# Row sums of a graph-attention kernel's exponentials: eight matmul tiles of 64 rows by 32 columns in two PSUM banks, in place of four of 128 rows by 32

## The chip, the cores and the metric

The kernel runs on one core of one Trainium2 chip. The metric is the device time of one execution in microseconds (us); lower is better. The time before is the median of three runs, and one further execution was taken by the hardware profiler.

## The reference

Two graph layers over x (8 batches, 2048 nodes, 256 features) with one adjacency matrix (2048 x 2048). Everything is float32. What matters here is the first layer's attention: softmax is taken separately inside each chunk of 256 keys, and the weighted values of the eight chunks are added.

```python
# layer 0, on h = relu(layernorm(x)); q, k, v in 4 heads of 64
scores = einsum('bhnd,bhjcd->bhnjc', q, kc) / sqrt(64)     # j: 8 chunks, c: 256 keys
scores = where(mask == 0, -10, clip(scores, -10, 10))
attn = softmax(scores, axis=-1)                            # over the 256 keys of a chunk
ctx = einsum('bhnjc,bhjcd->bhnd', attn, vc)
out = layernorm(ctx @ Wo.T + bo + h) * gamma + beta        # x = x + out
# layer 1, on h = relu(layernorm(x)): additive attention over all 2048 keys, then x = x + elu(...)
```

## The kernel before

One function, `layers`, writes the instructions of both layers in an order laid down by hand; each engine then runs its own queue in that order, and semaphores tie the queues together. Work beside the main line (projections, transposes, layer norms) is held in generators, and `advance` and `tick` hand a few of them out per step. So the place of an instruction in its queue is fixed when the program is built.

**The steps of the first layer.** There are 256 steps: 8 batches, 4 blocks of 512 queries, and 8 pairs of a 512-key block and a pair of heads. A 512-key block holds two chunks of 256 keys (`c` = 0 and 1), and is worked in four parts `t`; in a part, rows 0 to 63 of a tile are 64 keys of chunk 0, rows 64 to 127 are 64 keys of chunk 1. The loop at the end works on step n, n+1 and n+2 at once, in the order `S0 E0 S1 E1 C0 S2 E2 M0 C1 S3 E3 C2 C3 B0 A0`:

- S (`scores`, matmul L529): the scores of step n+2, four matmuls on 64x64 quarters of the TensorE array, into a `pair` of PSUM banks; then VectorE clips and masks them into `E` (L537). E (`exponential`, L543) is the exponential on ScalarE.
- C (`weigh`, matmul L551): step n's exponentials times the values, again on 64x64 quarters, into the banks `both`.
- A: `add_up` (matmul L564) takes the sum over keys of step n+1's exponentials, which GpSimd has first added over the four parts (`added`, L921 and L923) into one tile of 128 rows; `divide` copies the sums out of PSUM on ScalarE (L575) and sends them with a small DMA into 128 partitions (L577, tile `sum`).

After the order, `accumulate` multiplies step n's weighted values with the reciprocal sums `r` on VectorE (L603, L605), `invert` takes the reciprocals for step n+1 (L582) and writes them to DRAM (`inv`, L584), `spread` reads them back to all partitions (`r`, L591), and `advance` emits work beside it: mostly `narrow` (L162, four 32-column tiles over all 128 rows) or transposes (`flip`, L171).

**The sums before the change.** A matmul names a tile of the array by the partitions of its operands and of its output. In `add_up` four matmuls use all 128 rows and 32 columns each, for two heads times two halves of 256 queries. Their weights are `both_of`, 128 x 32: rows 0 to 63 have ones in columns 0 to 15, rows 64 to 127 in columns 16 to 31, so that one tile keeps the two chunks apart. The eight wanted rows come out at partitions 0, 16, 32 and so on of one bank (`sums`, 128 x 256), and L577 takes every sixteenth row. A float32 matmul appears in the trace as two weight loads and two matmuls.

The second layer (from L981 on) uses 32-column tiles of 128 rows (L1003, L1014) and has no part in the change.

Of the kernel before, what the change touches and what calls it, by code (L numbers as in the profile page):

```python
# [8 lines left out]
F32 = mybir.dt.float32  # L9
# [7 lines left out]
P = 128  # L17
# [34 lines left out]
def layers(  # L52
# [18 lines left out]
    nc = tc.nc  # L71
# [12 lines left out]
    big = ctx.enter_context(tc.tile_pool(name="big", bufs=2))  # L84
# [10 lines left out]
    def pair(dtype=F32):  # L95
        n = QB if dtype == F32 else 2 * QB
        return psum.tile([P, 2, n], dtype, tag="big", name="big", bufs=3)

    def banks(name):
        return [psum.tile([P, QB], F32, tag=f"both{k}", name=name) for k in range(2)]  # L100
# [5 lines left out]
    def heads_tile(name, tag, bufs=2):  # L106
        return big.tile([P, 2, QB], F32, tag=tag, name=name, bufs=bufs)
# [10 lines left out]
    def fetch_all():  # L118
        while loads:
            nc.sync.dma_start(*loads.pop(0))  # L120
# [99 lines left out]
    def advance(all_of=True):  # L220

        moved = all_of and tick()
        for steps_of in list(aside):
            got = next(steps_of, aside)
            if got is aside:
                aside.remove(steps_of)
            moved = moved or got is not False
            if got is None:
                break
        return moved  # L230

    def drain(until=lambda: False):
        while not until() and advance():
            pass
# [178 lines left out]
    def batch(b):  # L413
        qkv[b] = ([], [], [])
        rstd, off = norm_of[b] = norms()
        mv = small.tile([P, NKT, 2], F32, tag="mv", name="mv", bufs=1)
        ready, turned = [], []

        def slot():

            n = here[0]
            while b and here[0] < n + 1:
                yield False

        def statistics():

            for blk in range(NQB):
                while (
                    here[0] < first_of(b) + slot_of(b, TURN[blk]) - (5 if b > 1 else 7) or len(turned) < blk
                    if b  # L430
                    else blk > len(turned) + 2
                ):
                    yield False
                xb = load(x[b], blk)
                if b == 0:
                    fetch_all()
                yield True
                for two in range(NT // 2):
                    yield from slot()
                    for t in (2 * two, 2 * two + 1):  # L440
                        row_stats(nc, small, mv[:, blk * NT + t, :], xb[:, t, :])
                roots(mv, rstd, off, slice(blk * NT, (blk + 1) * NT))
                yield from slot()
                ready.append(xb)

        quiet.append(statistics())
        if b == 0:
            yield from opening(ready, turned)
            return
        hTs = {}  # L450
        for blk in range(NQB):
            yield from turning(b, blk, ready, turned, hTs)
            for name in "qkv" if blk == 2 else "kvq":
                yield from item(b, name, blk, hTs[blk], *qkv[b])
# [50 lines left out]
    def bias():  # L505
        spread_bv = big.tile([P, 2, P], F32, tag="h", name="spread_bv", bufs=3)
        nc.vector.tensor_copy(spread_bv, bcast(bv_col, 2, P))
        yield from later()
        ps = aux()[:, :F]
        for s in range(2):  # L510
            nc.tensor.matmul(
                ps, spread_bv[:, s, :], wT["o"][:, s, :], start=(s == 0), stop=(s == 1)
            )
        nc.vector.scalar_tensor_tensor(brow["o"], ps, float(NCH), brow["o"], ALU.mult, ALU.add)
        yield

    both_of = const.tile([P, 32], F32, tag="both_of", name="both_of")
    nc.gpsimd.memset(both_of, 0.0)
    for c in range(2):
        nc.gpsimd.memset(both_of[64 * c : 64 * c + 64, 16 * c : 16 * c + 16], 1.0)  # L520

    def scores(qb, blk, t, hp, qs, ks):

# [21 lines left out]
    def weigh(hp, t, e, v, both):  # L545

        for hh in range(2):
            mine = slice((2 * hp + hh) * DH, (2 * hp + hh + 1) * DH)
            for c in range(2):
                own = slice(64 * c, 64 * c + 64)  # L550
                nc.tensor.matmul(  # L551
                    both[c][64 * hh : 64 * hh + 64, :],
                    v[own, t, mine],
                    e[own, hh, :],
                    start=(t == 0),
                    stop=(t == NT - 1),
                )

    def add_up(added, sums):

        for hh in range(2):
            for half in range(2):
                n = 2 * hh + half
                nc.tensor.matmul(  # L564
                    sums[32 * n : 32 * n + 32, :],
                    both_of,
                    added[:, hh, half * 256 : (half + 1) * 256],
                    start=True,
                    stop=True,
                )  # L570

    def divide(sums):

        s = big.tile([P, 256], F32, tag="s", name="s", bufs=1)
        nc.scalar.copy(s, sums)  # L575
        got = small.tile([P, 16], F32, tag="sum", name="sum")
        nc.sync.dma_start(got, s[0:P:16, :].rearrange("n (j i) -> n j i", i=16))  # L577
        return got

    def invert(got):  # L580
# [303 lines left out]
    def fill(qb):  # L884

        while here[0] < (B - 1) * NQB * NCH + qb * NCH + NCH - 1:
            yield False
        for two in range(NKT // 2):
            fill_pair(qb, two)
            yield True  # L890

    def last_batch():
        yield from batch(B - 1)
        aside.append(sources_of(W, a))
        yield from preparation(0)
# [5 lines left out]
    def mask_part():  # L901
        next(mask_compares, None)
        next(mask_turns, None)

    def prepared(step):


        b, qb, c = step
        blk, hp = divmod(c, 2)
        drain(lambda: (qb, blk // 2) in made and b in qkv and len(qkv[b][1]) > blk and len(qkv[b][0]) > qb)  # L910
        qs, ks, _ = qkv[b]
        for t in range(NT):
            e = scores(qb, blk, t, hp, qs, ks)
            yield e
            exponential(e)
            yield None
# [11 lines left out]
    for n in range(-2, len(steps)):  # L928
        here[0] = n
        if n >= 0:  # L930
            b, qb, c = steps[n]
            blk, hp = divmod(c, 2)
            if n == NT:
                aside.append(bias())
            b1 = 1 if n == 1 else b + 2 if (qb, c) == (NQB - 1, NCH - 2) else B
            if b1 < B:
                aside.append(batch(b1) if b1 + 1 < B else last_batch())
            if b == B - 1 and c == NCH - 2 and qb < NQB - 1:
                aside.append(fill(qb))
            drain(lambda: len(qkv[b][2]) > blk)  # L940
            both = banks("both")
            v = qkv[b][2][blk]
        coming = prepared(steps[n + 2]) if n + 2 < len(steps) else iter(())
        inside = -1 <= n < len(steps) - 1
        weights[n + 2] = []
        for kind, t in ORDER:
            if kind in "SE":
                weights[n + 2] += [e for e in (next(coming, None),) if e is not None]
            elif kind == "A":
                if inside:  # L950
                    sums = pair()[:, 0, :256]
                    add_up(totals.pop(n + 1), sums)
                    got = divide(sums)
            elif kind == "B":
                if 0 <= n < 4:
                    advance(False)
            elif kind == "M":
                mask_part()
            elif n >= 0:
                weigh(hp, t, weights[n][t], v, both)  # L960
        weights.pop(n, None)
        if n + 2 < len(steps):
            totals[n + 2] = added(weights[n + 2])
        if n >= 0:
            if c == 0:
                accs[qb] = heads_tile("acc", "acc")
            accumulate(accs[qb][:, hp, :], both, r, blk == 0)
            if c == NCH - 1:
                finish(b, qb, accs[qb])
        held = invert(got) if inside else None  # L970
        if n >= 0:
            tick()
        if inside:
            r = spread(held)
        fetch_all()
        for _ in range({-2: 5, 3: 2}.get(n, 3 if n < NQB * NCH else 2)):
            advance(n < 0)
        mask_part()
# [204 lines left out]
    for s, (k, jt) in enumerate(rounds):  # L1183
# [44 lines left out]
        for entry in [entry for entry in due if entry[0] <= s]:  # L1228
            due.remove(entry)
            _, j, blocks = entry  # L1230
# [296 lines left out]
```

## Time and profile before

| what | value |
|---|---|
| time, median of 3 runs (lowest to highest) | 3971.54 us (3970.2 to 3981.95) |
| profiled execution: time; span from first to last instruction | 3974.03 us; 3972.2 us |
| busy share of the span: PE, DVE, ACT, POOL | 97%, 86%, 64%, 85% |
| mean granted TensorE clock | 0.992 |
| first and last matmul of L564 | 49.1 us, 2586.2 us |
| L564: instructions, mean of one | 2048, 392 ns |
| L575, copy of the sums: instructions, mean of one | 256, 366 ns |

PE is TensorE's matmuls, PEld its weight loads, DVE is VectorE, ACT ScalarE, POOL GpSimd, SP SyncE, which issues DMAs. A matmul's end is modelled, so the distance between the starts of matmuls tells more than their busy time. A line "A <- B" means that A waited for B or reads B. The chain of waits is followed back from the last instruction, at each step to what released it.

### The profile page before, as it was taken

The numbers are of one execution on the slowest core, as the hardware profiler recorded it, in microseconds if no ns is written. First come the engines' busy times: TensorE is split into PE (matmuls) and PEld (weight loads), VectorE is DVE, ScalarE is ACT, GpSimd is POOL, SyncE is SP. The second block draws the span as 40 slices with busy tenths as digits, with TensorE's granted clock in tenths as the row PEclk, the third lists the DMA queues.
The fourth block names the chain that finished last, engine by engine and source line by source line (L and its number), as shares of the span: only waits on it lengthen the run. The fifth ranks groups of instructions, "written<-read, shape, count | busy, mean of one in ns | idle before, by whom it ended". The sixth has DMA issues, their size and how long they took to land.

```text
span 3972.2 us, 93255 instructions
## 1 busy us (share of the span) xinstructions
PE 3846.7 (97%) x38454; PEld 1359.6 (34%) x38454; DVE 3409.6 (86%) x3920; ACT 2527.0 (64%) x3635; POOL 3380.8 (85%) x1763
## 2 busy tenths in 40 slices
PE   7899999999999999999999998989999999999997
PEld 2233333333333333333333333323333333333332
DVE  5778888888888888888888877879999999999998
ACT  7756556666566566656665656556766667676666
POOL 4678899999899899999999988858778778788887
PEclk9999999999999999999999999999999999999999
DMA  7723333333333333333333333322223122232222
GB/s 184 175 74 82 82 82 88 82 83 93 83 82 85 84 84 82 90 84 80 86 90 81 77 91 84 88 75 78 57 66 76 47 74 67 55 72 62 55 55 50
DMA packets 379442, 324.33 MB, mean 82 GB/s; under 512 B 261504, under 2 KB 329856, under 8 KB 379008
## 3 DMA queue, kind: packets, MB, share of 16 engines
q1 hardware_dynamic: 373312, 301.24, 29.8%
q0 software_dynamic: 4608, 16.78, 1.2%
q8 instruction: 304, 4.98, 0.5%
q14 instruction: 130, 1.06, 0.1%
q10 hardware_dynamic: 1088, 0.26, 0.0%
HBM read 271.26 MB, written 36.18 MB: 77 GB/s over the span
## 4 chain that ended last, share of the span: by engine, by line
PE 64%; DMA 13%; DVE 9%; POOL 5%; ACT 4%; issue 3%; SPq 1%; DVEq 0%; POOLq 0%; ACTq 0%
PE acc L1003 17%; PE big L529 15%; PE both L551 13%; PE big L162 7%; PE den L1014 6%; DMA r<-inv 5%; POOL t L1214 3%; DMA sum<-s 3%; DMA inv<-sum 3%; DVE E L537 3%; PE rest L162 2%; PE big L564 2%; DVE e L993 2%; ACT E L543 2%; DMA x<-in_x_dram 2%
## 5 line engine op out<-in xcount | busy, mean ns | idle before, releaser
L543 ACT ACTIVATE E<-E 128x1024 f32<-128x1024 f32 x1024 | 1081.8, 1058 | 683.1 <-DVE E L537 623.8
L537 DVE SCALAR_TENSOR_TENSOR E<-big,limit 128x1024 f32<-128x1024 f32 x1024 | 1198.6, 1214 | 91.5 <-PE big L529 85.9
L923 POOL TENSOR_TENSOR add<-add,E 128x1024 f32<-128x1024 f32 x512 | 1216.3, 2376 | 40.3 <-ACT E L543 0.2
L993 DVE SCALAR_TENSOR_TENSOR e<-near,far,limit 128x2048 f32<-128x2048 f32 x512 | 1166.6, 2341 | 30.7 <-issue 16.1
L529 PE MATMUL big<-qT,kT 64*64 64x512 f32 x8192 | 1069.6, 601 | 34.7 <-DVE E L537 11.8
L551 PE MATMUL both<-E,v 64*64 64x512 f32 x8192 | 1075.1, 592 | 9.4 <-DVE acc L605 6.2
L1214 POOL TENSOR_TENSOR t<-t,e 128x1024 f32<-128x1024 f32 x384 | 911.7, 2420 | 188.3 <-PE den L1014 99.7
L1003 PE MATMUL acc<-e,qn 128*32 128x512 f32 x8192 | 979.1, 595 | 11.8 <-DVE e L993 11.6
L921 POOL TENSOR_TENSOR add<-E 128x1024 f32<-128x1024 f32 x256 | 629.2, 2458 | 209.1 <-ACT E L543 208.7
L1173 ACT ACTIVATE t<-e,quot 128x1024 f32<-128x1024 f32 x384 | 419.8, 1141 | 200.3 <-PE den L1014 148.8
L551 PEld LDWEIGHTS both<-E,v 64*64 64x64 f32 x8192 | 341.8, 134 | 588.0 <-issue 502.1
L529 PEld LDWEIGHTS big<-qT,kT 64*64 64x64 f32 x8192 | 293.6, 133 | 613.0 <-issue 342.8
L1003 PEld LDWEIGHTS acc<-e,qn 128*32 128x32 f32 x8192 | 270.6, 110 | 554.9 <-issue 467.6
L603 DVE TENSOR_TENSOR both<-both,r 128x512 f32<-128x512 f32 x448 | 310.8, 694 | 165.1 <-DMA r<-inv 118.9
L605 DVE TENSOR_TENSOR acc<-both,acc 128x512 f32<-128x512 f32 x448 | 309.8, 692 | 15.3
L1014 PE MATMUL den<-t,for_sums 128*32 128x512 f32 x1536 | 230.6, 593 | 7.7 <-POOL t L1214 7.6
L564 PE MATMUL big<-add,both_of 128*32 128x256 f32 x2048 | 164.0, 392 | 0.0
L1014 PE MATMUL den<-e,for_sums 128*32 128x512 f32 x1024 | 149.9, 592 | 0.0
L582 DVE RECIPROCAL sum<-sum 128x16 f32<-128x16 f32 x256 | 63.7, 249 | 87.8 <-DMA sum<-s 83.8
L162 PE MATMUL big<-hT,wk 128*32 128x512 f32 x1024 | 125.1, 610 | 9.9 <-ACT hT L179 9.9
L1131 ACT ACTIVATE z<-z,dens 128x64 f32<-128x64 f32 x496 | 124.6, 334 | 2.0 <-DVE z L1115 2.0
L162 PE MATMUL big<-wv,hT 128*32 128x256 f32 x2048 | 123.5, 383 | 1.4 <-ACT hT L179 1.3
(142 smaller groups left out, 3060.7 us busy)
## 6 DMA issues: line engine op xcount, KB each, us to landing
r<-inv SPq DMA_DIRECT2D x512, 256.0 KB
x<-in_x_dram SPq DMA_DIRECT2D x96, 512.0 KB
es<-er SPq DMA_DIRECT2D x64, 512.0 KB
adj_in<-in_adj_dram SPq DMA_DIRECT2D x32, 512.0 KB
x<-o POOLq DMA_DIRECT2D x32, 512.0 KB, 4.4
x<-x SPq DMA_DIRECT2D x32, 512.0 KB
xh<-x SPq DMA_DIRECT2D x128, 128.0 KB
out_dram<-xh SPq DMA_DIRECT2D x124, 128.0 KB
```

The lines of the kernel that those rows point to most:

```text
L162: nc.tensor.matmul(to[32 * j : 32 * j + 32], lhsT[:, n : n + 32], rhs, start=start, stop=stop)
L529: nc.tensor.matmul(ps[64 * c : 64 * c + 64, hh, :], ks[blk][own, hp, keys : keys + 64], qs[qb][own, hp, :], start=True, stop=True,)
L537: nc.vector.scalar_tensor_tensor(e, ps, -0.5, bcast(limit[:, qb, NT * blk + t, :], 1, 2), ALU.max, ALU.min)
L543: nc.scalar.activation(e, e, AF.Exp, scale=0.25 * EDGE)
L551: nc.tensor.matmul(both[c][64 * hh : 64 * hh + 64, :], v[own, t, mine], e[own, hh, :], start=(t == 0), stop=(t == NT - 1),)
L921: nc.gpsimd.tensor_tensor(total, tiles[0], tiles[1], ALU.add)
L923: nc.gpsimd.tensor_tensor(total, total, e, ALU.add)
L993: nc.vector.scalar_tensor_tensor(e, near, far[:, jt, h : h + 1], limit[:, :, jt, :], ALU.max, ALU.min)
L1003: nc.tensor.matmul(acc[part][32 * blk : 32 * blk + 32, :], qn[jt // NT][:, jt % NT, own], e[:, blk, :], start=(jt == 0), stop=(jt == NKT - 1),
L1014: nc.tensor.matmul(den[32 * blk : 32 * blk + 32, :], for_sums[:, jt, :], blocks[blk], start=first, stop=last,)
L1173: nc.scalar.activation(t, e[:, 2 * half : 2 * half + 2, :], AF.Copy, scale=shared[b][4][:, jt // 2, h : h + 1],)
L1214: nc.gpsimd.tensor_tensor(ts[half], ts[half], now[:, 2 * half : 2 * half + 2, :], ALU.add)
```

## The change

`both_of` becomes all ones. Each of the four matmuls of `add_up` becomes two, one for each chunk: 64 rows of weights and of data, 32 columns, the same 256 columns of data, and the two row halves write two different banks of the pair. `divide` copies both banks (512 elements a partition in place of 256), and the DMA takes every thirty-second row, which now holds both chunks.

```diff
     both_of = const.tile([P, 32], F32, tag="both_of", name="both_of")
-    nc.gpsimd.memset(both_of, 0.0)
-    for c in range(2):
-        nc.gpsimd.memset(both_of[64 * c : 64 * c + 64, 16 * c : 16 * c + 16], 1.0)
+    nc.gpsimd.memset(both_of, 1.0)
...
                 n = 2 * hh + half
-                nc.tensor.matmul(
-                    sums[32 * n : 32 * n + 32, :],
-                    both_of,
-                    added[:, hh, half * 256 : (half + 1) * 256],
-                    start=True,
-                    stop=True,
-                )
+                for c in range(2):
+                    own = slice(64 * c, 64 * c + 64)
+                    nc.tensor.matmul(
+                        sums[32 * n : 32 * n + 32, c, :],
+                        both_of[own, :],
+                        added[own, hh, half * 256 : (half + 1) * 256],
+                        start=True,
+                        stop=True,
+                    )
...
-        s = big.tile([P, 256], F32, tag="s", name="s", bufs=1)
-        nc.scalar.copy(s, sums)
+        s = big.tile([P, 512], F32, tag="s", name="s", bufs=1)
+        nc.scalar.copy(s.rearrange("p (c q) -> p c q", c=2), sums)
         got = small.tile([P, 16], F32, tag="sum", name="sum")
-        nc.sync.dma_start(got, s[0:P:16, :].rearrange("n (j i) -> n j i", i=16))
+        nc.sync.dma_start(got, s[0:P:32, :].rearrange("n (j i) -> n j i", i=16))
...
-                    sums = pair()[:, 0, :256]
+                    sums = pair()[:, :, :256]
```

The rows of `got` and of everything behind it stay as they were. On each engine the order of the instructions stays the same too, but for the four matmuls that become eight and two memsets fewer on GpSimd.

## The prediction

> **What bounds the kernel now.** I read the busy shares and the chain of waits first, then the first layer alone, because L564 runs only from 49 to 2586 us.
>
> ```profile
> PE 3846.7 (97%) x38454; PEld 1359.6 (34%) x38454; DVE 3409.6 (86%) x3920; ACT 2527.0 (64%) x3635; POOL 3380.8 (85%) x1763
> PE 64%; DMA 13%; DVE 9%; POOL 5%; ACT 4%; issue 3%; SPq 1%; DVEq 0%; POOLq 0%; ACTq 0%
> 60.00:2600.00 2540.00, 2471.05 (x24829) 892.96 (x24824) 2097.90 (x3043) 1561.79 (x2004) 2261.83 (x1186) 0.99 0.34 89
> by line: PE big L529 23.0%; PE both L551 20.8%; PE big L162 10.6%; DMA r<-inv 8.0%; DMA inv<-sum 4.2%; DMA sum<-s 4.2%; DVE E L537 3.7%; issue 3.4%; PE big L564 3.2%; ACT E L543 2.5%; DVE both L603 2.2%; DMA x<-in_x_dram 2.1%; DVE acc L605
> ```
>
> The third line is the window 60 to 2600 us (span, then busy time of PE, weight loads, DVE, ACT, POOL); the fourth is the chain inside it. TensorE is busy for 2471 of 2540 us, so it has at most 69 us of slack, and over half of the chain lies on it. Most of the rest of the chain is the path of the sums: the small DMA into `sum`, the one to `inv`, and the reading of `r`. Time added to TensorE therefore mostly reaches the end; so does time added to the path of the sums, in those steps where that path is the late one.
>
> The next view is the one the forecast rests on: one pass of L564 and its neighbours in the timeline of PE.
>
> ```profile
> 1001.51 0.61 PE L529 MATMUL big<-qT,kT 64*64 64x512 f32 x4
> 1001.94 1.90 PE L551 MATMUL both<-E,v 64*64 64x512 f32 x16
> 1003.77 0.64 PE L564 MATMUL big<-add,both_of 128*32 128x256 f32 x8
> 1004.23 1.91 PE L162 MATMUL big<-wo,acc 128*32 128x256 f32 x32
> 1006.07 0.66 PE L171 MATMUL big<-ident,h 128*128 128x128 f32 x4
> ```
>
> Four matmuls run at once and start as a burst. From the first line to the second, one burst of 512 columns takes 0.43 us, so one of 256 columns takes 0.215. L551 has four bursts, 1.72 us, and would end at 1003.66; L564 starts at 1003.77, 0.11 late, though nothing it needs is late. Its own two bursts should take 0.43 and take 0.46. L162 then follows with no loss: its eight bursts would end at 1005.95. L171 starts at 1006.07, again 0.12 late. Time is lost where the tile's form changes (64x64 to 128x32, then 128x32 to 128x128), and not between L564 and L162, which share one form. In the trace's records the medians from start to start are 539 ns from L551's last burst to L564 against 429 inside L551 (110 lost), 330 from L564 or L162 to L171 against 216 (114 lost), 329 from L162 to L529's 64x64 (113 lost), and 202 from L171 to L529 against 109 (93 lost). The weight loads say why:
>
> ```profile
> 1003.77 0.16 PEld L564 LDWEIGHTS big<-add,both_of 128*32 128x32 f32 x8 [0.81 <-issue]
> 1004.01 0.35 PEld L162 LDWEIGHTS big<-wo,acc 128*32 128x32 f32 x8
> ```
>
> L162's weights load at 1004.01, under L564's second burst and 0.22 us before their own matmul. L564's load only at 1003.77, with the matmul. A change of form thus empties the array and bares a load: 240 ns instead of 216 for the first burst, 24 more.
>
> **What the change removes and adds on TensorE.** Before, a pass has the form change 64x64 to 128x32 ahead of it. Behind it come L162 or L791 (also 128x32) in 228 of 256 passes, counted in the trace, and another form in the other 28. After, 64x64 goes to 64x32, and 64x32 to 128x32.
>
> - Entry: 64x64 to 64x32 changes the columns alone. The nearest row is the change of columns alone from 128x32 to 128x128, which costs 114 ns, as much as the changes of rows and columns together. Bounds 0 and 114; I take 110 plus 24, as before. Difference 0.
> - Exit, 228 passes: 64x32 to 128x32 changes the rows alone, which no row shows. Every change that is shown costs 93 to 114, so bounds 0 and 114; I take 114, and 24 for L162's first load. In the other 28 it is paid before and after.
> - Streaming: eight tiles of half the height are the whole array, so 16 matmuls still need two rounds of 256 columns, 0.43 us. Two things could spoil that. The rate of issue: the change needs 16 matmuls in 0.43 us, and L791, in the fence below, issues 16 in four bursts 0.109 apart (medians of the starts), the same rate. And the two row halves writing two banks at once: L529 already does so with 64x64 tiles. I take 0; the upper bound, four tiles at a time, is 0.43 a pass.
> - Start: four tiles begin 0.02 us apart in all (a burst of L529 spans 0.61 where one matmul has 0.59), about 7 ns each. In a stream of one form this hides; ahead of a form change the last tile's end counts. Four more tiles: 0.027 us.
>
> ```profile
> 2465.53 0.62 PE L791 MATMUL big<-hT,wa 128*32 128x128 f32 x16
> L575 ACT COPY s<-big 128x256 f32<-128x256 f32 x256 | 93.7, 366 | 5.5 <-PE big L564 5.3 <-ACT E L543 0.2
> L357 ACT COPY v<-big 128x512 f32<-128x512 f32 x64 | 36.8, 577 | 47.6 <-PE big L162 47.6
> L179 ACT COPY hT<-big 128x512 f32<-128x512 f32 x72 | 41.9, 583 | 79.5 <-PE big L171 79.3
> DVE both L603 <- DMA r<-inv: 118.9, 98, 6.5
> DVE sum L582 <- DMA sum<-s: 83.8, 83, 5.8
> ```
>
> Together a pass grows by 0.114 + 0.024 + 0.027 = 0.165 us in 228 steps and by 0.027 in 28: 37.6 + 0.8 = 38.4 us if all of it counts. L564 has 3.2% of the chain in the window, 81 us; at 0.57 a pass in the chain that is 143 of 256 passes, which alone give 143/256 of 38.4 = 21 us. In the other 113 the addition first eats slack, and all the slack that TensorE has is 69 us, most of it in a few long waits. So 21 to 38 us, nearer the upper end: 32.
>
> The Trainium skill has a rule on this, in TensorEngine Tiling (Array Packing), under Tiling Modes: going to another tiling mode, not merely to another tile, drains TensorE. It speaks against this change, and by it the exit costs as much as the rows above; a gate that looked at rows alone would leave the entry free.
>
> **The copy.** L575 grows from 256 to 512 elements: from 0.366 to about 0.58 us, by L357 and L179, so 0.217 more. ACT has the room (1562 of 2540 us busy), but the copy stands ahead of `sum`'s DMA; L575 itself hardly waits for the matmul (5.5 us in all), since the exponentials queued before it on ACT end later. Behind the copy on ACT stand `hT`, `kT` and `v` (L179, L378, L357), which already wait for their matmuls. DVE waits for `sum` 83 times, with L603 and L537 of later steps queued behind that. The chain passes through `sum`'s DMA 45 times (counted in its pieces): 45 x 0.217 = 10 us. If this cover vanished in all 256 steps it would be 56.
>
> **The DMA and the rest.** L577 still moves 128 pieces, now from four partitions instead of eight, which no row shows. Undisturbed, `sum` takes 1.79 us in the chain and `inv`, read from 128 partitions, 1.39; I bound the effect by that difference, 0.4 us either way, 18 us over 45 passes, and take 0, since count and size of the pieces stay. Nothing else moves in any queue: SP's order is the same, and GpSimd loses two memsets before 50 us, next to nothing. `pair` was taken whole before too, so no new wait for a bank arises.
>
> **The sum.** 32 + 10 gives about 41 us. Against the profiled execution: 3974.0 + 41 = 4015. That execution stands 2.5 us above the median of the runs, so for the median 3971.5 + 41 = 4012.5; I say 4012. The bounds of this case are 21 + 10 and 38 + 10, with 18 either way for the DMA: 3985 to 4037.
>
> **Rivals.**
>
> - *Only the rows decide.* If a change of columns alone is free, each entry wins 0.134 and each exit loses 0.165 (0.027 in 28): 228 x 0.031 - 28 x 0.107 = +4 us, with the copy +14: about 3985. For it: no row shows a change from 64x64 to 64x32. Against: 128x32 to 128x128 keeps the rows and loses 114 ns. Chance 0.10.
> - *The other side: neither change drains.* If 64-row tiles follow 64x64 without emptying the array, and 128x32 can follow them tile by tile, a pass loses its 0.134 and gains 0.027: -0.107, over 143 to 256 passes -15 to -27 us. The copy gives back up to 10, so about 3955, between 3944 and 3967. It decides only where both borders of L564 are free; with one drain left it is gone. For it: 64x32 tiles nest in the 64x64 ones. Against: all four kinds of change in the trace cost about 0.1. Chance 0.06.
> - *The eight tiles do not run together.* Two rounds of four per pass of weights: +0.43 a pass, over 143 to 256 passes +62 to +110 on top of the forecast, about 4095. Against it stand L529's two banks and L791's rate. Chance 0.08.
> - The forecast: 0.76.
>
> **How the numbers follow.** The range 3981 to 4037 takes in the forecast's bounds and the middle of the first rival; the other two, 0.14, are left out. About 0.3%, 12 us, can be told from no change. Faster by more is most of the second rival: 0.05. Same is the rest of it and half of the first: 0.08. Slower is the remainder: 0.87.
>
> **What would show it.** In the profile after: L564 has 4096 matmuls of form 64x32; it starts 0.11 us after L551's last burst should end; its first L162 weights no longer load ahead, and L162 starts some 0.6 us after L564 in place of 0.46; L575's mean is near 580 ns; DVE waits a little longer for `sum`. I am wrong if L162's weights load under L564's last burst, if L564 starts 0.43 after the burst before, or if its own rounds are 0.43 apart.

## The result and the profile after

The changed kernel takes 4003.16 us (median of four runs, 3999.69 to 4009.24) against 3972.95 us for the kernel before (four runs): ratio 1.0077, 95% interval 1.0066 to 1.0089, so 0.77% or some 30 us slower. The profiled execution has a span of 4003.1 us.

In the changed file the scores' matmul stands at L527 (L529 before), the weighing at L549 (L551), the clipping at L535 (L537) and the exponential at L541 (L543); lines from L564 on keep their numbers. The timeline of PE, around one pass:

```profile
1011.58 1.90 PE L549 MATMUL both<-E,v 64*64 64x512 f32 x16
1013.40 0.66 PE L564 MATMUL big<-add,both_of 64*32 64x256 f32 x16
1014.00 1.93 PE L162 MATMUL big<-wo,acc 128*32 128x256 f32 x32
1015.86 0.66 PE L171 MATMUL big<-ident,h 128*128 128x128 f32 x4
```

L549's four bursts of 0.43 us would end at 1013.30; L564 starts 0.10 late, as before. But L162 now starts 0.60 us after L564, where it was 0.46, and its eight bursts take 1.86 where they took 1.84. The medians of the starts in the trace's records: from L549's last burst to L564 539 ns, to the nanosecond what it was; L564's first round 240, as before; its second round to L162's start 353 in place of 216; L162's first round 240 in place of 216. The weight loads of the same pass:

```profile
1013.40 0.18 PEld L564 LDWEIGHTS big<-add,both_of 64*32 64x32 f32 x16 [0.81 <-POOL o L679]
1013.99 0.37 PEld L162 LDWEIGHTS big<-wo,acc 128*32 128x32 f32 x12 [0.41 <-issue]
```

L162's weights load at 1013.99, with their matmul at 1014.00 and no longer 0.22 us ahead of it. A border, in what follows, is a place where one tile form follows another. By the late starts and the bare loads, L564 now has one on both sides.

The groups of instructions, L564 first of the kernel before, then the two of the changed kernel:

```profile
L564 PE MATMUL big<-add,both_of 128*32 128x256 f32 x2048 | 164.0, 392 | 0.0
L564 PE MATMUL big<-add,both_of 64*32 64x256 f32 x4096 | 170.1, 389 | 0.1
L575 ACT COPY s<-big 128x512 f32<-128x512 f32 x256 | 148.9, 582 | 6.7 <-PE big L564 5.1
```

The waits of DVE (us in total, times, longest) in the first layer; the first line is the kernel before, 60 to 2600 us, the other two the changed one, 60 to 2630 us:

```profile
DVE sum L582 <- DMA sum<-s: 78.0, 82, 5.4
DVE both L603 <- DMA r<-inv: 130.4, 103, 5.7
DVE sum L582 <- DMA sum<-s: 103.9, 147, 5.3
```

Twice the matmuls take hardly more busy time (170 us in place of 164): all eight tiles run together. The copy has grown from 366 to 582 ns, and DVE now waits 147 times for the sums in place of 82, for 104 us in place of 78 (the 83 waits and 83.8 us of the prediction are those of the whole span).

In its first-layer window the chain has the same shape, with more of it on TensorE:

```profile
by line: PE big L527 25.5%; PE both L549 23.5%; PE big L162 13.0%; DMA r<-inv 4.9%; DVE E L535 3.9%; PE big L564 3.9%; issue 3.5%; DMA sum<-s 3.4%; DMA inv<-sum 3.2%; ACT E L541 2.5%; DMA x<-in_x_dram 1.4%; DVE both L603 1.4%; DVE acc L605 
```

L564 holds 3.9% of 2570 us here. By the starts, TensorE's addition is 228 x (353 + 240 - 216 - 216 = 161 ns) plus 28 x 23 ns, 37.4 us.

### The profile page after: what moved, and what is told of

It reads as the page before. It is cut to its first block, busy times and chain, and to the rows that moved or that the text cites. A ratio compares the mean times of both kernels' runs of the same rounds, so it can differ in the third digit from the quotient of the medians.

```text
span 4003.1 us, 97348 instructions
## 1 busy us (share of the span) xinstructions
PE 3880.6 (97%) x40502; PEld 1350.4 (34%) x40502; DVE 3409.9 (85%) x3920; ACT 2591.5 (65%) x3635; POOL 3375.4 (84%) x1761
## 4 chain that ended last, share of the span: by engine, by line
PE 70%; DMA 9%; DVE 7%; ACT 5%; POOL 4%; issue 3%; SPq 1%; DVEq 0%; POOLq 0%; ACTq 0%
PE acc L1003 18%; PE big L527 16%; PE both L549 15%; PE big L162 8%; PE den L1014 6%; DMA r<-inv 3%; POOL t L1214 3%; DVE E L535 3%; PE big L564 2%; PE rest L162 2%; DMA sum<-s 2%; DMA inv<-sum 2%; ACT E L541 2%; DMA x<-in_x_dram 1%; DVE e L993 1%
## 5 line engine op out<-in xcount | busy, mean ns | idle before, releaser
L541 ACT ACTIVATE E<-E 128x1024 f32<-128x1024 f32 x1024 | 1081.4, 1057 | 669.4 <-DVE E L535 615.9
L535 DVE SCALAR_TENSOR_TENSOR E<-big,limit 128x1024 f32<-128x1024 f32 x1024 | 1198.4, 1215 | 75.5 <-PE big L527 70.0
L527 PE MATMUL big<-qT,kT 64*64 64x512 f32 x8192 | 1071.6, 601 | 27.4 <-DVE E L535 9.7
L549 PE MATMUL both<-E,v 64*64 64x512 f32 x8192 | 1074.7, 591 | 10.2 <-DVE acc L605 7.9
L549 PEld LDWEIGHTS both<-E,v 64*64 64x64 f32 x8192 | 343.4, 133 | 586.8 <-issue 496.2
L527 PEld LDWEIGHTS big<-qT,kT 64*64 64x64 f32 x8192 | 295.9, 133 | 601.5 <-issue 342.6
L564 PE MATMUL big<-add,both_of 64*32 64x256 f32 x4096 | 170.1, 389 | 0.1
L575 ACT COPY s<-big 128x512 f32<-128x512 f32 x256 | 148.9, 582 | 6.7 <-PE big L564 5.1
L162 PE MATMUL big<-hT,wk 128*32 128x512 f32 x1024 | 127.9, 622 | 10.3 <-ACT hT L179 10.3
L162 PE MATMUL big<-wv,hT 128*32 128x256 f32 x2048 | 125.3, 387 | 1.2 <-ACT hT L179 1.2
```

The costliest lines, as they stand in the source:

```text
L162: nc.tensor.matmul(to[32 * j : 32 * j + 32], lhsT[:, n : n + 32], rhs, start=start, stop=stop)
L527: nc.tensor.matmul(ps[64 * c : 64 * c + 64, hh, :], ks[blk][own, hp, keys : keys + 64], qs[qb][own, hp, :], start=True, stop=True,)
L535: nc.vector.scalar_tensor_tensor(e, ps, -0.5, bcast(limit[:, qb, NT * blk + t, :], 1, 2), ALU.max, ALU.min)
L541: nc.scalar.activation(e, e, AF.Exp, scale=0.25 * EDGE)
L549: nc.tensor.matmul(both[c][64 * hh : 64 * hh + 64, :], v[own, t, mine], e[own, hh, :], start=(t == 0), stop=(t == NT - 1),)
```

## The experiments

Four explanations are told apart. Theory 1 is the prediction's sum: TensorE's added time at L564's border to L162, and the larger copy on the path of the sums. Theory 2 has the copy covered. The rival has the copy carry the loss. Theory 3 has the 64x32 tiles cost something of their own. Each ratio is to the kernel before on the same chip. Three chips were used, which ran it at 3957 to 3958 us, so 1% is 40 us. A price in us is taken from the ratio; in brackets stands its 95% interval.

### The parts of the change alone

`e1_copy_alone`:

```diff
-        s = big.tile([P, 256], F32, ...)
-        nc.scalar.copy(s, sums)
+        s = big.tile([P, 512], F32, ...)
+        nc.scalar.copy(s.rearrange("p (c q) -> p c q", c=2), bcast(sums, 1, 2))
...
-        ... s[0:P:16, :].rearrange(
+        ... s[0:P:16, :256].rearrange(
```

> The kernel before with the larger copy alone: the one bank of sums is copied twice into a tile of 512 elements, and the DMA reads the first half; TensorE's work is untouched. The copy should take 0.58 in place of 0.366 us. Theory 1 (the prediction's sum, both terms on the path): about +10 us. Theory 2 (the larger copy is covered, and what is missing from the forecast of +41 is this term): 0 to +3 us. Rival (the copy carries the loss, TensorE's additions vanish in slack): +20 to +30 us.

Measured: ratio 1.0030 (1.0018 to 1.0043), +12 us (7 to 17). The copy takes 579 ns. It is not covered, and the forecast's 10 us lie inside the interval. Theory 2 falls.

`e2_tiles_alone`, against the changed kernel:

```diff
-        s = big.tile([P, 512], F32, ...)
-        nc.scalar.copy(s.rearrange("p (c q) -> p c q", c=2), sums)
+        s = big.tile([P, 256], F32, ...)
+        nc.scalar.copy(s, sums[:, 0, :])
...
-        ... s[0:P:32, :].rearrange(
+        ... s[0:P:16, :].rearrange(
```

> The changed kernel with the divide step of before: only the first bank of sums is copied (256 elements) and the DMA reads every sixteenth row, so both chunks are divided by the first chunk's sums. TensorE has all of the change, ACT and the DMA none. Theory 1: +20 us (30 less the copy's 10). Theory 2: +28 to +32 us, the whole of the change. Rival (the copy carries it): 0 to +10 us.

Measured: 1.0082 (1.0069 to 1.0096), +32 us (27 to 38). TensorE's part alone costs the 32 us that the prediction gave it, and the copy does not carry the loss. Theory 1 as written for this run, +20, is missed: it took the parts to add up to the whole. Theory 2's +28 to +32 is met, though theory 2 fell with e1. But 32 and 12 make 44, and the whole change costs 30: that became the question of the second set.

### TensorE's time without a change of form

`e3_pe_time_96` and, with 256 in place of 96, `e4_pe_time_256`:

```diff
     def add_up(added, sums):
+        for n in range(4):
+            nc.tensor.matmul(
+                sums[32 * n : 32 * n + 32, :96],
+                both_of,
+                added[:, n // 2, (n % 2) * 256 : (n % 2) * 256 + 96],
+                start=True,
+                stop=True,
+            )
```

> The kernel before plus four more matmuls of the same form per pass, of 96 columns, overwritten by the real ones: about 0.16 us of TensorE a pass (0.22 if weight loads set the pace) without a change of form. If the change costs by TensorE time alone, this costs the same per us: 256 x 0.16 = 41 us of TensorE at the rate of the change (30 measured of 37 added), so +31 to +35; at 0.22 a pass some +45. If a change of form costs something beyond the time at the border (theory 3), it is clearly less per added us than the change.

> As the run before, with 256 columns: 0.43 us a pass, 111 us in all. If slack absorbs a fixed amount (7 to 10 us), about +102; if it absorbs a share (a fifth), about +89; if everything counts, +111.

Measured: 1.0083 (1.0070 to 1.0097), +33 us, and 1.0215 (1.0202 to 1.0228), +85 us (80 to 90). In the timeline of e3 the added matmuls are L562, the old ones L572:

```profile
1006.18 0.37 PE L562 MATMUL big<-add,both_of 128*32 128x96 f32 x8
1006.37 0.61 PE L572 MATMUL big<-add,both_of 128*32 128x256 f32 x8
1006.80 1.91 PE L162 MATMUL big<-wo,acc 128*32 128x256 f32 x32
```

From L562 to L162 it is 0.62 us in place of 0.46: by the medians of its starts 166 ns more a pass, 42.5 us in all, of which 33 or 77% show (65 to 90% by the interval). In e4 85 of 110.6 show, also 77%. In e2 32 of 37.4 show, 87% (73 to 102%). So at this place slack absorbs a share and not a fixed amount, which would have left +102 in e4. The 87% are not told apart from the 77%: theory 3 is not needed here, but the 10% between them, some 4 us, cannot be excluded. The last pair below tests it at another place.

### Do copy and TensorE's time add up?

`after_again` is the changed kernel without an edit.

> The changed kernel once more, beside the runs of this call. By the first measurement +30 us (ratio 1.0077). If copy alone (+12) and tiles alone (+32) simply added up, it would be +44, ratio 1.011.

Measured: 1.0087 (1.0070 to 1.0105), +34 us; with the first measurement, 30 to 34. With the +10 of the copy's second measurement below, the parts make 42 to 44, so 8 to 14 us have to be explained.

`e5_old_dma`, against the changed kernel:

```diff
-        ... s[0:P:32, :].rearrange(
+        ... s[0:P:16, :256].rearrange(
```

> The changed kernel, but the DMA into sum reads every sixteenth row and the first 256 elements, as before (so both chunks are divided by the first one's sums). Only the DMA's reading of four partitions is undone. Overlap theory (the larger copy and TensorE's time delay the same steps, so the larger of them counts): the same as the changed kernel, +28 to +33. Rival (the DMA from four partitions gives back what the copy costs): +40 to +46.

Measured: 1.0098 (1.0081 to 1.0115), +39 us (32 to 46): between the two expectations, and both reach into its interval.

`e6_copy_and_pe` has the edits of e1 and e3 together.

> The kernel before with the larger copy and with the four added matmuls of 96 columns, which cost +12 and +33 alone; no change of form, no new DMA. Overlap theory: +32 to +37. Rival (they add up, and the changed kernel is saved by something else): +43 to +47.

Measured: 1.0112 (1.0093 to 1.0130), +44 us (37 to 51). The sum of the two alone is 1.0113. They add up, and the overlap theory, +32 to +37, falls but for the edge of the interval. What is left is the DMA that reads four partitions, or chance. So it was tried without the tiles: `e8_copy_dma4` is e1 with one more edit, beside `e9_copy_again`, which is e1.

```diff
-        ... s[0:P:16, :256].rearrange(
+        ... s[0:P:32, :].rearrange(
```

> The kernel before with the larger copy and the DMA of the change: it reads every thirty-second row, 512 elements, so it brings the first chunk's sums twice. TensorE's work is that of before. Theory 1 (the DMA from four partitions gives back what is missing in the changed kernel, about 12 us): 0 to +4. Theory 2 (it gives nothing; it lands 0.06 us later in the traces): +12 to +16, no less than the copy alone beside it.

> The larger copy alone once more, as the other side of the run before: +12 us by its first measurement (ratio 1.003, interval 1.0018 to 1.0043).

(In these two, theories 1 and 2 are new ones, on the DMA alone.) Measured: 1.0012 (1.0002 to 1.0022) with the new DMA, +5 us (1 to 9); 1.0024 (1.0015 to 1.0034) without it, +10 us. The intervals of the two ratios overlap, but both are taken against the same runs of the kernel before, and the two can be compared directly: the means of their eleven runs each differ by 4.6 us (95% interval 1 to 8). In the same way e5 and the changed kernel beside it, six runs each, differ by 6.0 us (1 to 11). So the new DMA gives back some 5 us in both exchanges, at the edge of what these runs can tell.

What changes in the DMA can be read from the traces. Its issue on SP is shorter, 581 ns in place of 642 (medians), and yet the reciprocal that waits for it starts 1861 ns after the issue began in place of 1796 (smallest values). The records of its packets, in the traces of the kernels before and after, show what lies behind it: 128 packets of 64 bytes both times, of which the first starts 1217 ns after the issue began in place of 1278, and the last ends after 1544 ns in place of 1475 (medians). At most 5 packets are under way at once in place of 11 (medians too), and 4 packets of 4 bytes go with them in place of 8. So the data start earlier and land later, with about half as many packets side by side. Why a sum that lands 65 ns later should save time stays open. The issue on SP, the first line before and the second after:

```profile
L577 SPq DMA_DIRECT2D sum<-s x256: 631/642/777, 53.8 to 2587.1; - x128
```

```profile
L577 SPq DMA_DIRECT2D sum<-s x256: 573/581/717, 55.1 to 2617.8; - x128
```

### The border itself: another place

`e10_mid_before` and `e11_mid_after` move the pass, in the kernel before and in the changed one:

```diff
-"S0 E0 S1 E1 C0 S2 E2 M0 C1 S3 E3 C2 C3 B0 A0"
+"S0 E0 S1 E1 C0 S2 E2 M0 C1 S3 E3 C2 A0 C3 B0"
```

> The kernel before with its four 128x32 tiles, the pass placed between C2 and C3, so that 64x64 tiles stand on both sides. It gains nothing and pays one change of form more a step: 0.113 for 128x32 to 64x64 and about 0.05 for the first load there, 0.16 x 256 = 42 us of TensorE, at the fifth to quarter that slack absorbed so far: +31 to +36.

> The changed kernel with the pass placed between C2 and C3 too. Here both forms stand between 64x64 tiles, and the one has no neighbour in common that the other lacks. Theory 1 (the change costs by the border to L162): only the start of eight tiles (0.023 a pass, 6 us) and the copy (12) are left, so +5 to +18 over the run before. Theory 3 (64x32 tiles cost by themselves, wherever they stand): +30 over it, as at the old place. Rival of the prediction (changes of columns alone are free between 64-row forms): it is faster than the run before, by 60 us for both borders.

Measured: 1.0193 (1.0175 to 1.0210), +76 us, and 1.0219 (1.0203 to 1.0235), +87 us. The timeline of PE in e10, then in e11:

```profile
1005.42 1.04 PE L551 MATMUL both<-E,v 64*64 64x512 f32 x8
1006.39 0.64 PE L564 MATMUL big<-add,both_of 128*32 128x256 f32 x8
1006.96 1.09 PE L551 MATMUL both<-E,v 64*64 64x512 f32 x8
1007.98 1.93 PE L162 MATMUL big<-wv,hT 128*32 128x256 f32 x32
```

```profile
1009.47 1.04 PE L549 MATMUL both<-E,v 64*64 64x512 f32 x8
1010.43 0.66 PE L564 MATMUL big<-add,both_of 64*32 64x256 f32 x16
1011.02 1.09 PE L549 MATMUL both<-E,v 64*64 64x512 f32 x8
```

Between 64x64 tiles both forms lose alike: 0.57 us from L564 to what follows, and 0.59. The changed kernel stands 12.7 us above the other by the medians (7 to 16 by the means), within the 5 to 18 of theory 1, where at the old place it was 30 to 34. So what the change costs beyond the copy and the later start is the border to L162, which four 128-row tiles do not have, and theory 3 falls. The copy's 10 to 12 us, the start's 6 and the 5 that the DMA gives back make 11 to 13. The rival of the prediction, free changes of columns, would have shown L564 at 1010.33 and not 1010.43.

The expectation for e10 was less than half of what came, by an error of counting: taking the pass away from L162 adds not one border but two, one behind the pass (0.113 and 0.051 for the load) and one ahead of L162 (0.110 and 0.024), which L564 had paid before. 228 x 0.298 us with some 3 us for the other passes is 71 us, and 76 (69 to 83) came: by the count, no share was absorbed here. That need not be the price of the borders alone, since after the move DVE also waits more for the last weighing, which now stands behind the pass (first line before, 60 to 2600 us, second e10, 60 to 2640 us):

```profile
DVE both L603 <- PE both L551: 26.0, 65, 0.9
DVE both L603 <- PE both L551: 150.1, 145, 1.3
```

`e7_sums_early` puts the pass after C1, to give the sums a start:

```diff
-"S0 E0 S1 E1 C0 S2 E2 M0 C1 S3 E3 C2 C3 B0 A0"
+"S0 E0 S1 E1 C0 S2 E2 M0 C1 A0 S3 E3 C2 C3 B0"
```

> The kernel before with its four tiles, but the pass of sums placed after C1 in the order in place of the end, so its copy goes ahead of the last exponential on ACT. TensorE pays a change of form into the pass and out of it, and still the one ahead of L162: about 0.16 us more a step, +33 us by the runs so far. The sums come 2 to 3 us earlier, which can give back at most TensorE's remaining slack, 69 us. Theory (the path of the sums is what the slack waits for): between -20 and +10 us. Rival (the waits are for other things, or the pass then waits for GpSimd's additions): +25 us or more.

Measured: 1.0157 (1.0139 to 1.0176), +62 us (55 to 70): a miss by the same count, 71 us of borders, and on the rival's side. 62 of 71 is 87%, no less than the shares of added TensorE time above, so the runs do not show that the earlier sums gave anything back. The waits of DVE show that the path of the sums was indeed relieved; the first line is the kernel before, the others e7:

```profile
DVE E L537 <- PE big L529: 85.9, 196, 3.7
DVE E L537 <- PE big L529: 240.8, 300, 4.3
DVE sum L582 <- DMA sum<-s: 35.3, 10, 5.8
```

DVE waits for `sum` 10 times in place of 82, but for TensorE's scores 241 us in place of 86. In this run, relieving the path bought nothing that can be told, with TensorE as the bound. No version tried beats the kernel before.

## Why the prediction was right or wrong

The direction, the mechanism and the range were right: 4003 lies between 3981 and 4037, and 30 us came where 41 were forecast. The signs named in the prediction all came: L564 0.10 us late, L162's weights bare, 0.60 us from L564 to L162, 582 ns for the copy, more waits for `sum`.

- **Entry, 0 difference.** Right to the nanosecond, 539 both times. A change of columns alone costs the same 110 ns, and the first rival falls on this row; the second needed both borders free and had neither. The Trainium skill (TensorEngine Tiling (Array Packing), Tiling Modes) states that another tiling mode drains TensorE. This trace agrees: 110 ns for a change of columns alone, and 137 ns, the later start of eight tiles included, for a change of rows alone. No row of before showed either together with a 64-row form.
- **Exit.** Forecast 114 + 24 + 27 ns for the border, the bare load and the later start of eight tiles. Measured 137 for border and start together and 24 for the load: 161 in place of 165. (Counted again, 229 passes have L162 or L791 at once behind them; it changes nothing.)
- **Streaming.** Forecast 0: the first round takes 240 ns as before, and the rounds do not split. The third rival falls.
- **How much of it reaches the end.** Forecast 32 of 38.4, chosen between the chain's share and the whole and not worked out. The tiles alone gave 32 of 37.4; that the choice is met so closely is in part luck, since the interval is 27 to 38. The chain's share, 143 of 256 passes, was too low a guide, as was thought: 77 to 87% of added TensorE time showed.
- **The copy.** Forecast 582 ns and 10 us; measured 582 ns, and 12 and 10 us. The count of the chain's passes through the sums' DMA, 45, came out well here, but it is a rough guide: in the profiles of e1 and e9, which are one kernel, it is 38 and 57, and the same kind of count was too low for TensorE.
- **The DMA**, the one step mis-sized: taken as 0 within 18 either way, since neither the count nor the size of the packets changes. It gives back some 5 us. Parts and whole differ by 8 to 14 us (32 with 10 or 12 against 30 to 34), so 5 is about half of that; the rest lies inside the intervals of the parts. No other cause was found.

The range would have held without the 18 us allowed for the DMA, but only just: the other bounds alone begin at 4002.5. Among the chances, half of the first rival and the rest of the second make 0.06, where 0.08 stands for "same".

## What to carry to other kernels

On TensorE, price the border of a group of small matmuls by both its neighbours: a tile form that is cheap by itself costs a border, here some 0.11 us, and a bare weight load, here 0.024 us and more, wherever its neighbour has another form, in rows or in columns. Here the old form shared its form with what came behind it, and the new one with nothing. When a pass is moved, count the borders it leaves as well as those it gets, since a pass may have been paying for its neighbour.

## What was not expected of the hardware

That about four fifths of small additions to TensorE would show (77% twice, 87% once), with DVE, ACT and GpSimd all waiting often, was seen in no row of before. And a DMA of the same 128 pieces of 64 bytes was issued 61 ns faster from four partitions than from eight, while its packets, about half as many side by side, took 326 ns from first start to last end in place of 196, and what waited for it started 65 ns later.
